# Local attention in a reordered round, and norms centred with the tokens on the partitions

## The chip, the cores and the metric

The kernel runs on one NeuronCore of a Trainium2 chip. The metric is the device time of one execution in microseconds (us), lower is better. A core has a matrix engine (PE, with weight loads shown apart as PEld), a vector engine (DVE), a scalar engine (ACT), a GpSimd engine (POOL) and a queue that issues transfers (SP). Each works through its own list of instructions; semaphores tie them together. Matrix products land in PSUM[...]; everything else lives in SBUF or in DRAM.

## The reference

Two blocks run one after the other on `x` of shape (2, 2048, 128), all in float32. Each block modulates a layer norm, adds an attention (kind A), modulates again and adds a stack of local-attention layers (kind B):

```python
h = layernorm(x) * (1 + ca) + sa;  x = x + ga * attn(h)
h = layernorm(x) * (1 + cb) + sb;  x = x + gb * local_layers(h)

# one local-attention layer (first block: 6 layers, 16 heads, window 32;
#                            second block: 2 layers, 8 heads, window 64; head size 64)
h = shift_token(x)                     # second half of the features comes from the token before
q, k, v = split(h @ Wqkv)
q, k = rotary_xpos(l2norm(q) * qs, l2norm(k) * ks)
o = softmax(mask(8 * q @ [k_prev_window, k_window].T)) @ [v_prev_window, v_window]
x = x + o @ Wo
h = layernorm(shift_token(x)) * g + b
a, gate = split(h @ W1 + b1)
x = x + (a * gelu(gate)) @ W2 + b2
```

The attention of the first block is a chunked delta-rule attention; that of the second is a causal linear attention with two layer norms and a feed-forward network of its own. Only the local-attention layers and the linear attention are touched by the change.

## The kernel before

The work is in three stages. `modulation` and `l0_attention` (up to about 530 us of the profile) do the first attention under an order written out by hand; the change does not touch them. `local_models` does all eight local-attention layers, with the linear attention of the second block threaded through the end of the sixth layer and the start of the seventh. In `local_models` a scheduler sets the final order of each engine's instructions from the order of the source, the data dependencies and the free buffers, so a round's instructions may interleave differently from round to round. Features lie on the partitions for the residual streams `hs[0]` and `hs[1]` (128 features by tokens).

A tile is 128 tokens of one of the two sequences, so a layer has 32 tiles, and the main loop runs one round per tile over a software pipeline. In round `i`, with `j = i + 3`:

- `scores(i + 1)` computes the masked scores into a two-bank PSUM tile (`wide`, line 991, mask in line 982), then DVE takes the maximum `mx` (line 999) and the difference `sm` (1001). `weights_exp` runs the exponential on ACT (1008), `weights_norm` the sum `rs` and its reciprocal on DVE (1015, 1016) and the product on POOL (1017).
- `project(j, 0)` and, for 16 heads, `project(j, 1)` compute 1,024 columns of queries and keys each into a `wide` tile (line 871). ACT squares them (`sq`, 873), DVE forms the two halves of the rotation, `r` (881) and `t` (886), and POOL adds them (892). After the last of a tile's projections DVE sums the squares (897) and runs `rsqrt_quick` (lines 167 to 180, last result `rq_y`), which uses the projection's own PSUM bank as scratch; POOL then scales `r` by `rq_y` (904). For 8 heads one projection holds queries and keys.
- `keys_first_(i)` turns the weights of tile `i` so that keys lie on partitions (`ps_pT`, line 1026), and ACT copies them (1027).
- `values(i + 2)` computes values (`ps_v`, line 951), ACT copies them into `vn`, and SP moves them window by window into `v2`, which has two buffers.
- `mix(i)` multiplies weights and values (`ps_o`, line 1043), ACT copies the outputs `on` (1049).
- `turn(i + 2, u)` turns queries and keys (`ps_turn`, line 923), ACT copies them to `qT` and `kT`, and the last window of the tile before is copied in front of the keys (line 934, or a memset in 932).
- `turn_out(i)` turns the outputs (`ps_oT`, line 1059), and `project_out(i)` multiplies them with `Wo` (`ps_y`, line 1071) and adds to the residual on DVE (1077).

`wide` tiles rotate through two pairs of banks, all others (`bank`) through four single banks. After every fourth tile of a sequence `feed_forward` queues six steps, of which each round runs two: `centre`, `variance`, `scale`, `gate`, `up`, `down`. `centre` multiplies 512 tokens with a centring matrix (line 1096), so features stay on the partitions, and squares the result on ACT (1098). `variance` sums the squares over the features with four one-column products on PE (1107) and takes the inverse root (DVE 1112, POOL 1114). `scaled` spreads that root over the partitions with four transposes on PE (1120), and DVE multiplies (1123). The linear attention and the last residual of a model queue steps in a second list, of which each round runs up to six (`lstep`); the linear attention calls `centre` and `variance` four times per 512 tokens, and `scaled` three times. The order of a round in the source is:

```python
            if i >= 0:
                keys_first_(i)
            if 0 <= i + 2 < n:
                values(i + 2)
            lstep()
            if i >= 0:
                mix(i)
            if 0 <= i + 2 < n:
                for u in range(len(layers[tiles[i + 2][0]][0].units)):
                    turn(i + 2, u)
            lstep()
            if i >= 0:
                turn_out(i)
```

In it stand both projections before `keys_first_(i)`.

Of the kernel before, what the change touches and what calls it, by code (L numbers as in the profile page):

```python
# [11 lines left out]
F32 = mybir.dt.float32  # L12
# [3 lines left out]
ALU = mybir.AluOpType  # L16
# [56 lines left out]
def tile_kernel(ctx: ExitStack, tc: tile.TileContext, a: dict, out: bass.AP):  # L73
# [634 lines left out]
    def local_models(mA, mB, hs0):  # L708
# [12 lines left out]
        def bank(name):  # L721
            return psT.tile([128, 512], F32, tag="T", name=f"ps_{name}")
# [139 lines left out]
        def project(i, u):  # L862
# [31 lines left out]
            if u == len(units) - 1:  # L894
# [7 lines left out]
                for v in range(len(units)):  # L902
# [2 lines left out]
                        rv, rv, bc(y[:, 16 * v:16 * v + 16].unsqueeze(2), (128, 16, DH)), ALU.mult  # L905
                    )

        def turn(i, u):

            g, b, t = tiles[i]  # L910
            m, _ = layers[g]
            W, NPR = m.W, m.NPR
            if u == 0:
                q = wk.tile([128, 1024], F32, name="qT")
                st[i]["q"] = q[:, 0:NPR * 128].rearrange("p (c i) -> p c i", c=NPR)
                k = wk.tile([128, 1280], F32, name="kT", bufs=3)
                st[i]["k"] = k[:, 0:NPR * (W + 128)].rearrange("p (c i) -> p c i", c=NPR)
            r = st[i].pop(("r", u))
            for e, (s, pb) in enumerate(m.units[u]):
                p = bank("turn")  # L920
                for c in range(4):
                    cs = slice(512 * e + 128 * c, 512 * e + 128 * c + 128)
                    nc.tensor.transpose(p[:, c * 128:(c + 1) * 128], r[:, cs], ident)  # L923
                pv = p.rearrange("p (c i) -> p c i", c=4)
                if s == 0:
                    nc.scalar.copy(st[i]["q"][:, 4 * pb:4 * pb + 4, :], pv)
                else:
                    nc.scalar.copy(st[i]["k"][:, 4 * pb:4 * pb + 4, W:W + 128], pv)  # L928
            if u == len(m.units) - 1:
                k = st[i]["k"]  # L930
                if t == 0:
                    nc.gpsimd.memset(k[:, :, 0:W], 0.0)
                else:
                    nc.scalar.activation(
                        k[:, :, 0:W], m.last_k[b][:, :, 128:128 + W], AF.Identity, scale=m.back
                    )
                m.last_k[b] = k

        def values(i):
            g, b, t = tiles[i]  # L940
# [150 lines left out]
                lsteps.pop(0)()  # L1091


        def centre(S, x, pool, keep):
            p = bank("c")
            nc.tensor.matmul(p, lhsT=cen, rhs=x, start=True, stop=True)  # L1096
            S["sq"] = pool.tile([128, 512], F32, name="fsq")
            nc.scalar.activation(S["sq"], p, AF.Square)
            if keep:
                S["xc"] = pool.tile([128, 512], F32, tag="t1", name="xc")  # L1100
                nc.scalar.copy(S["xc"], p)

        def variance(S, pool):
            p = bank("var")
            sq = S.pop("sq")
            for j in range(4):
                nc.tensor.matmul(  # L1107
                    p[:, j:j + 1], lhsT=sq[:, j * 128:(j + 1) * 128], rhs=onesm[:, 0:1],
                    start=True, stop=True,
                )  # L1110
            ve = pool.tile([128, 4], F32, name="fve")
            nc.vector.tensor_scalar(ve, p[:, 0:4], 1e-5, None, ALU.add)
            S["rt"] = pool.tile([128, 4], F32, name="frt")
            nc.gpsimd.tensor_tensor(S["rt"], ve, bc(nhalf, (128, 4)), ALU.pow)

        def scaled(S, x, out):
            p = bank("r")
# [121 lines left out]
        def linear(b, k):  # L1239
# [13 lines left out]
                pass  # L1253

            def a3():
                xc = S.pop("xc")
                scaled(S, xc, xc)
                h = S["h"] = lw.tile([128, 512], F32, name="h")
                nc.scalar.activation(
                    h, xc, AF.Identity, bias=mB[:, 0, b:b + 1], scale=mB[:, 1, b:b + 1]  # L1260
                )


# [132 lines left out]

            def f3():
                n0 = k * 512
                xc = S.pop("xc")
                scaled(S, xc, xc)  # L1400
                for lo, sh in ((0, 0), (64, 1)):
                    nc.scalar.activation(
                        hs0[lo:lo + 64, b, n0 + sh:n0 + sh + 512], xc[lo:lo + 64, :],
                        AF.Identity, bias=mB[lo:lo + 64, 3, b:b + 1],
                        scale=mB[lo:lo + 64, 4, b:b + 1],
                    )
                ready.add((b, k))
# [46 lines left out]
        for i in range(-3, n):  # L1454
            j = i + 3
            lstep()
            if 0 <= i + 1 < n:
                scores(i + 1)
                weights_exp(i + 1)
                weights_norm(i + 1)  # L1460
            more = False
            if j < n:
                g, b, t = tiles[j]
                jj = j % per
                nu = len(layers[g][0].units)
                more = g < last
                if g == second and t % 4 == 0:
                    while (b, t // 4) not in ready:
                        lstep()
                project(j, 0)  # L1470
                if more and jj == 4:
                    load_proj(g + 1, 0)
                if more and jj == 6 and g + 1 == second:
                    models[1].consts()
                if jj == 6 and g == second - 1:
                    linear_consts()
                if more and jj == 8:
                    factors(g + 1)
                    if 2 == 2:
                        load_out(g + 1)  # L1480
                if more and jj == 18:
                    load_ff(g + 1)
                if more and jj == 22:
                    fold_ff(g + 1)
                if more and jj == per - 1:
                    load_proj(g + 1, 1)
                lstep()
            step()
            if j < n and nu == 2:
                project(j, 1)  # L1490
                if more and jj == per - 1 and g + 1 < second:
                    load_proj(g + 1, 2)
            if j < n and b == B - 1 and j + 1 < n:
                tables(*tiles[j + 1][::2])
            lstep()
            if i >= 0:
                keys_first_(i)
            if 0 <= i + 2 < n:
                values(i + 2)
            lstep()  # L1500
            if i >= 0:
                mix(i)
            if 0 <= i + 2 < n:
                for u in range(len(layers[tiles[i + 2][0]][0].units)):
                    turn(i + 2, u)
            lstep()
            if i >= 0:
                turn_out(i)
            step()
            lstep()  # L1510
            if i >= 0:
                g, b, t = tiles[i]
                project_out(i)
                if 2 == 1 and i % per == per - 1 and g < last:
                    load_out(g + 1)
                if t % 4 == 3:
                    feed_forward(g, b, t // 4)
# [74 lines left out]
```

## Time and profile before

| what | us |
|---|---|
| median of three runs | 5040.5 |
| lowest and highest | 5033.6, 5043.1 |
| the profiled execution, its own time | 5053.3 |
| its span, first to last instruction | 5051.4 |
| first attention ends, local layers begin | about 530 to 614 |
| layers of 16 heads alone | 614 to 3590 |
| 16 and 8 heads, mixed with linear attention | 3590 to 4404 |
| layers of 8 heads alone | 4404 to 4990 |

The profile shows one execution. A row has the engine, the source line, the operation, the tiles it writes and reads, its shape, and how often it occurs. A number in square brackets behind a row is the time for which the engine stood idle before it, and what released it. A float32 product appears in the trace as two records, a transpose as one.

### The profile page before, as it was taken

The numbers are of one execution on the slowest core, as the hardware profiler recorded it, in microseconds if no ns is written. First come the engines' busy times: TensorE is split into PE (matmuls) and PEld (weight loads), VectorE is DVE, ScalarE is ACT, GpSimd is POOL, SyncE is SP. The second block draws the span as 40 slices with busy tenths as digits, with TensorE's granted clock in tenths as the row PEclk, the third lists the DMA queues.
The fourth block names the chain that finished last, engine by engine and source line by source line (L and its number), as shares of the span: only waits on it lengthen the run. The fifth ranks groups of instructions, "written<-read, shape, count | busy, mean of one in ns | idle before, by whom it ended". The sixth has DMA issues, their size and how long they took to land.

```text
span 5051.4 us, 171478 instructions
## 1 busy us (share of the span) xinstructions
PE 4682.5 (93%) x75042; PEld 3190.3 (63%) x75042; DVE 3883.5 (77%) x6760; ACT 2796.3 (55%) x4645; POOL 2761.1 (55%) x1650
## 2 busy tenths in 40 slices
PE   5667799999999999999999999999999998999998
PEld 4445566666666666666666666666666665566565
DVE  6993488788887887788887788787767766688886
ACT  3323356666666665566665566566555654555554
POOL 3331366666665666566666666665544533355553
PEclk8777799999999999999999999999999999999999
DMA  2000222222222322232222322232222211111111
GB/s 76 1 1 24 83 69 66 63 71 74 70 63 63 82 70 63 62 81 72 63 64 65 81 67 64 64 82 64 52 53 54 54 44 36 41 46 48 53 54 40
DMA packets 222491, 295.63 MB, mean 59 GB/s; under 512 B 75657, under 2 KB 95409, under 8 KB 221745
## 3 DMA queue, kind: packets, MB, share of 16 engines
q1 hardware_dynamic: 221744, 284.67, 21.8%
q8 instruction: 592, 9.70, 0.8%
q14 instruction: 155, 1.26, 0.1%
HBM read 40.98 MB, written 10.75 MB: 10 GB/s over the span
## 4 chain that ended last, share of the span: by engine, by line
PE 75%; DVE 6%; ACT 4%; issue 2%; POOL 2%; DMA 0%; SPq 0%; ACTq 0%; POOLq 0%; DVEq 0%
PE ps_qk L871 15%; PE ps_y L1071 8%; PE ps_turn L923 8%; PE ps_o L1043 7%; PE ps_s L991 7%; PE ps_v L951 6%; PE ps_f L1141 6%; PE ps_oT L1059 4%; PE ps_pT L1026 4%; PE ps_fy L1166 3%; PE ps_var L1107 1%; PE ps_c L1096 1%; PE ps_s L982 1%; POOL r L892 1%; ACT sq L873 1%
## 5 line engine op out<-in xcount | busy, mean ns | idle before, releaser
L892 POOL TENSOR_TENSOR r<-r,t 128x1024 f32<-128x1024 f32 x448 | 1059.9, 2366 | 1162.4 <-DVE t L886 1075.2
L873 ACT ACTIVATE sq<-ps_qk 128x1024 f32<-128x1024 f32 x448 | 459.1, 1025 | 1369.4 <-PE ps_qk L871 1353.2
L904 POOL TENSOR_TENSOR r<-r,rq_y 128x1024 f32<-128x1024 f32 x448 | 845.5, 1905 | 268.0 <-DVE rq_y L180 267.1
L871 PE MATMUL ps_qk<-wp,hs 128*128 128x512 f32 x1792 | 883.6, 616 | 30.1 <-DVE rq_y L180 15.4
L886 DVE TENSOR_TENSOR t<-ps_qk,tb 128x1024 f32<-128x1024 f32 (+1 forms) x512 | 552.8, 1080 | 180.5 <-POOL r L892 180.4
L1017 POOL TENSOR_TENSOR sm<-sm,rs 128x1024 f32<-128x1024 f32 x256 | 488.0, 1906 | 293.6 <-DVE rs L1016 196.2
L881 DVE TENSOR_TENSOR r<-ps_qk,tb 128x1024 f32<-128x1024 f32 (+1 forms) x512 | 547.7, 1070 | 103.1 <-ACT sq L873 102.1
L897 DVE TENSOR_REDUCE ps_qk<-sq 128x16 f32<-128x1024 f32 x448 | 549.6, 1227 | 13.5
L871 PEld LDWEIGHTS ps_qk<-wp,hs 128*128 128x128 f32 x1792 | 311.6, 191 | 351.5 <-issue 260.2
L1071 PEld LDWEIGHTS ps_y<-oT,wo 128*128 128x128 f32 x3584 | 440.8, 193 | 122.4 <-issue 71.1
L1071 PE MATMUL ps_y<-oT,wo 128*128 128x128 f32 x3584 | 482.8, 282 | 18.7 <-ACT oT L1060 18.2
L923 PE MATMUL ps_turn<-ident,r 128*128 128x128 f32 x3584 | 470.6, 281 | 22.9 <-issue 12.0
L1043 PEld LDWEIGHTS ps_o<-v,pT 64*32 64x32 f32 (+1 forms) x26624 | 343.6, 108 | 226.9 <-ACT pT L1027 114.9
L951 PE MATMUL ps_v<-wp,hs 128*128 128x512 f32 x896 | 446.9, 598 | 5.9 <-ACT o L1436 3.7
L999 DVE TENSOR_REDUCE mx<-ps_s 128x16 f32<-128x1024 f32 (+1 forms) x256 | 312.9, 1222 | 166.4 <-PE ps_s L991 162.1
L1043 PE MATMUL ps_o<-v,pT 64*32 64x64 f32 (+1 forms) x26624 | 392.5, 222 | 41.0 <-ACT pT L1027 23.3
L923 PEld LDWEIGHTS ps_turn<-ident,r 128*128 128x128 f32 x3584 | 395.2, 143 | 54.4 <-issue 15.8
L991 PE MATMUL ps_s<-kT,qT 64*32 64x64 f32 (+1 forms) x26624 | 400.5, 230 | 3.9 <-ACT kT L928 3.2
L1049 ACT COPY on<-ps_o 128x512 f32<-128x512 f32 x448 | 244.4, 589 | 244.1 <-PE ps_o L1043 244.1
L991 PEld LDWEIGHTS ps_s<-kT,qT 64*32 64x32 f32 (+1 forms) x26624 | 330.1, 107 | 70.3 <-issue 37.3
L1141 PE MATMUL ps_f<-fx,w 128*128 128x512 f32 (+1 forms) x768 | 365.5, 600 | 2.6 <-DVE fx L1123 1.7
L1026 PEld LDWEIGHTS ps_pT<-ident,sm 128*128 128x128 f32 x2048 | 245.7, 142 | 149.6 <-issue 142.1
(266 smaller groups left out, 7693.6 us busy)
## 6 DMA issues: line engine op xcount, KB each, us to landing
v<-vn SPq DMA_DIRECT2D x1276, 128.0 KB
v<-vn SPq DMA_DIRECT2D x744, 64.0 KB
v<-vn SPq DMA_DIRECT2D x64, 256.0 KB
wp<-in_L_ffn_Wqkv SPq DMA_DIRECT2D x20, 512.0 KB
xD<-xb SPq DMA_DIRECT2D x24, 256.0 KB
xb<-xD SPq DMA_DIRECT2D x24, 256.0 KB
cs<-in_cos SPq DMA_DIRECT2D x128, 32.0 KB
cs<-in_sin SPq DMA_DIRECT2D x128, 32.0 KB
```

What stands on the lines that cost most here:

```text
L871: nc.tensor.matmul(pq[:, js], lhsT=hw, rhs=wts[g, u][:, js], start=True, stop=True)
L881: nc.vector.tensor_tensor(r[:, es].rearrange("p (h d) -> p h d", d=DH), pq[:, es].rearrange("p (h d) -> p h d", d=DH), bc(tb[:, 0, s].unsq ...
L886: nc.vector.tensor_tensor(t2[:, es].rearrange("p (h s d) -> p h s d", s=2, d=32), pq[:, es].rearrange("p (h s d) -> p h s d", s=2, d=32)[: ...
L892: nc.gpsimd.tensor_tensor(r, r, t2, ALU.add)
L897: nc.vector.tensor_reduce(pq[:, 16 * v:16 * v + 16], st[i].pop(("sq", v)).rearrange("p (h d) -> p h d", d=DH), AX.X, ALU.add,)
L904: nc.gpsimd.tensor_tensor(rv, rv, bc(y[:, 16 * v:16 * v + 16].unsqueeze(2), (128, 16, DH)), ALU.mult)
L923: nc.tensor.transpose(p[:, c * 128:(c + 1) * 128], r[:, cs], ident)
L951: nc.tensor.matmul(p, lhsT=hw, rhs=wv, start=True, stop=True)
L991: nc.tensor.matmul(sp[W * w:W * w + W, c0:c0 + 2 * W], lhsT=qT[64 * q:64 * q + 64, cc, W * w:W * w + W], rhs=kT[64 * q:64 * q + 64, cc, W ...
L1043: nc.tensor.matmul(po[s][W * w:W * w + W, co:co + 64], lhsT=pT[kp, q, c, W * w:W * w + W], rhs=v2[kp, w, co:co + 64], start=True, stop=True,)
L1071: nc.tensor.matmul(py[:, 0:128], lhsT=wts[g, "o"][:, c * NO + s, :], rhs=oT[:, s, c, :], start=(c + s == 0), stop=(c == 3 and s == NO - 1),)
L1141: nc.tensor.matmul(ps_[c][0:sz], lhsT=wts[g, "w1"][:, o:o + sz], rhs=S["x"], start=True, stop=True,)
```

## The change

The change does four things.

1. It reorders the round: weights of tile `i` are turned between the two projection halves (for 8 heads ahead of the only one), then come the outputs `mix(i)`, then `values(i + 2)`, `turn_out(i)` and last `turn(i + 2)`.
2. It takes the allocation of `kT` and the copy of the window before it out of `turn` into a function of its own, `halo`, called before the last projection half.
3. `centre` now takes the tokens as the stationary operand, in four products of 128 columns, so tokens lie on the partitions and features along the row. `variance` sums the squares with one DVE reduction along the row, in place of the four products.
4. Where the centred values are kept (two of the four norms of the linear attention), POOL scales them by the inverse root, and `normed` turns them back with four transposes, from which ACT reads directly; the transposes of the root and the DVE product fall away there. `scaled` stays for the other norms.

```diff
+        def halo(i):
+            g, b, t = tiles[i]
+            m, _ = layers[g]
+            W, NPR = m.W, m.NPR
+            k = wk.tile([128, 1280], F32, name="kT", bufs=3)
+            k = st[i]["k"] = k[:, 0:NPR * (W + 128)].rearrange("p (c i) -> p c i", c=NPR)
+            if t == 0:
+                nc.gpsimd.memset(k[:, :, 0:W], 0.0)
+            else:
+                nc.scalar.activation(
+                    k[:, :, 0:W], m.last_k[b][:, :, 128:128 + W], AF.Identity, scale=m.back
+                )
+            m.last_k[b] = k
...
         def centre(S, x, pool, keep):
             p = bank("c")
-            nc.tensor.matmul(p, lhsT=cen, rhs=x, start=True, stop=True)
+            for j in range(4):
+                js = slice(j * 128, (j + 1) * 128)
+                nc.tensor.matmul(p[:, js], lhsT=x[:, js], rhs=cen, start=True, stop=True)
...
         def variance(S, pool):
-            p = bank("var")
-            sq = S.pop("sq")
+            ve = pool.tile([128, 4], F32, name="fve")
+            nc.vector.tensor_reduce(
+                ve, S.pop("sq").rearrange("p (j d) -> p j d", j=4), AX.X, ALU.add
+            )
+            nc.vector.tensor_scalar(ve, ve, 1.0 / 128.0, 1e-5, ALU.mult, ALU.add)
+            rt = S["rt"] = pool.tile([128, 4], F32, name="frt")
+            nc.gpsimd.tensor_tensor(rt, ve, bc(nhalf, (128, 4)), ALU.pow)
+            if "xc" in S:
+                v = S["xc"].rearrange("p (j d) -> p j d", j=4)
+                nc.gpsimd.tensor_tensor(v, v, bc(rt.unsqueeze(2), (128, 4, 128)), ALU.mult)
+
+        def normed(S):
+            p = bank("n")
+            xc = S.pop("xc")
             for j in range(4):
-                nc.tensor.matmul(
-                    p[:, j:j + 1], lhsT=sq[:, j * 128:(j + 1) * 128], rhs=onesm[:, 0:1],
-                    start=True, stop=True,
-                )
...
+                js = slice(j * 128, (j + 1) * 128)
+                nc.tensor.transpose(p[:, js], xc[:, js], ident)
+            return p
...
-                project(j, 0)
+                if nu == 2:
+                    project(j, 0)
...
-                if more and jj == per - 1:
+                if nu == 2 and more and jj == per - 1:
                     load_proj(g + 1, 1)
                 lstep()
             step()
-            if j < n and nu == 2:
-                project(j, 1)
-                if more and jj == per - 1 and g + 1 < second:
+            if i >= 0:
+                keys_first_(i)
+            if 0 <= i + 2 < n:
+                halo(i + 2)
+            if j < n:
+                project(j, nu - 1)
+                if nu == 2 and more and jj == per - 1 and g + 1 < second:
                     load_proj(g + 1, 2)
-            if j < n and b == B - 1 and j + 1 < n:
-                tables(*tiles[j + 1][::2])
+                if nu == 1 and more and jj == per - 1:
+                    load_proj(g + 1, 1)
+                if b == B - 1 and j + 1 < n:
+                    tables(*tiles[j + 1][::2])
             lstep()
             if i >= 0:
-                keys_first_(i)
+                mix(i)
+            lstep()
             if 0 <= i + 2 < n:
                 values(i + 2)
             lstep()
             if i >= 0:
-                mix(i)
+                turn_out(i)
             if 0 <= i + 2 < n:
                 for u in range(len(layers[tiles[i + 2][0]][0].units)):
                     turn(i + 2, u)
-            lstep()
-            if i >= 0:
-                turn_out(i)
             step()
             lstep()
             if i >= 0:
```

## The prediction

> **What bounds the kernel now.** I read the page first: span, and how busy TensorE (PE) is.
>
> ```profile
> span 5051.4 us, 171478 instructions
> PE 4682.5 (93%) x75042; PEld 3190.3 (63%) x75042; DVE 3883.5 (77%) x6760; ACT 2796.3 (55%) x4645; POOL 2761.1 (55%) x1650
> ```
>
> It looks PE-bound. Next, busy time by stretch: layers of the 16-head model alone (614 to 3590 us), those mixed with linear attention (3590 to 4404), layers of the 8-head model alone (4404 to 4990).
>
> ```profile
> core 0: us, PE busy (x) PEld busy (x) DVE busy (x) ACT busy (x) POOL busy (x), PEclk, DMA share, GB/s
> 614.00:3590.00 2976.00, 2906.74 (x55644) 2002.27 (x55626) 2405.72 (x3921) 1810.71 (x2977) 1891.98 (x1098) 0.99 0.27 69
> 3590.00:4076.00 486.00, 462.05 (x7043) 316.90 (x7046) 347.82 (x602) 269.90 (x433) 237.35 (x142) 0.97 0.21 53
> 4076.00:4404.00 328.00, 294.70 (x2435) 194.56 (x2419) 207.00 (x449) 161.63 (x252) 124.33 (x85) 0.93 0.13 36
> 4404.00:4990.00 586.00, 555.83 (x5116) 353.19 (x5120) 492.71 (x1037) 340.79 (x547) 317.49 (x199) 1.00 0.18 50
> ```
>
> PE reads 95 to 98% in three of the four, but DVE stands at 81 and 84% in the first and the last. So I read single rounds in the timeline. A round without feed-forward work in the 16-head model:
>
> ```profile
> 2259.21 0.19 DVE L180 SCALAR_TENSOR_TENSOR rq_y<-ps_qk,rq_g 128x32 f32<-128x32 f32 x1
> 2259.74 1.98 PE L871 MATMUL ps_qk<-wp,hs 128*128 128x512 f32 x4
> ...
> 2262.83 1.22 DVE L881 TENSOR_TENSOR r<-ps_qk,tb 128x1024 f32<-128x1024 f32 x1 [0.32 <-ACT sq L873]
> ...
> 2268.87 1.22 DVE L886 TENSOR_TENSOR t<-ps_qk,tb 128x1024 f32<-128x1024 f32 x1 [1.32 <-POOL r L892]
> ...
> 2274.38 0.19 DVE L180 SCALAR_TENSOR_TENSOR rq_y<-ps_qk,rq_g 128x32 f32<-128x32 f32 x1
> ...
> 2274.81 0.70 PE L871 MATMUL ps_qk<-wp,hs 128*128 128x512 f32 x1
> ```
>
> To be seen: the round lasts 15.07 us (2259.74 to 2274.81), and each first projection starts only 0.24 to 0.34 us after DVE's `rq_y` has ended, because the inverse root is computed in the PSUM bank that this projection takes over. So the round is a loop over engines: projection, square (ACT), `r` and `t` (DVE), sum (POOL), the second `t` (which waited 1.32 us for POOL), two sums of squares, the root, the next projection. PE hides beside it. In the 8-head model the loop shows as a wait:
>
> ```profile
> 4601.90 0.17 DVE L180 SCALAR_TENSOR_TENSOR rq_y<-ps_qk,rq_g 128x16 f32<-128x16 f32 x1
> 4602.00 1.21 DVE L999 TENSOR_REDUCE mx<-ps_s 128x8 f32<-128x1024 f32 x1
> 4602.13 1.99 PE L871 MATMUL ps_qk<-wp,hs 128*128 128x512 f32 x4 [0.25 <-DVE rq_y L180]
> ...
> 4605.28 0.69 DVE L881 TENSOR_TENSOR r<-ps_qk,tb 128x512 f32<-128x512 f32 x1 [0.74 <-ACT sq L873]
> ```
>
> To be seen: `rq_y` comes first, and then projection and square (3.1 us) run while DVE does the softmax's `mx` and `sm` (2.5 us). That overlap is what I expect the change to break.
>
> **What the Trainium skill says.** (1) "PSUM — Partial Sum Buffer", Engine vs sequencer instructions: DVE, ACT and POOL queues are strict FIFO and matmuls start in program order; so an instruction that waits holds all behind it, and the issue order decides. (2) The same page, on bank collisions: two engines reading one bank are serialised by an added dependency. The trace agrees: `r` starts 0.04 us after `sq` ends. (3) "Perfetto Trace Analysis", Tensor Engine Instruction: a matmul's end is an estimate; so I count PE from start to start (two 512-column projections in four records: 1.82 us, not the 1.98 shown).
>
> **Prices, start to start, in us.** First projection pair 1.82, second 1.72, eight weight turns 0.87, values 0.86 to 0.95 each, outputs 1.51, query turns 1.80, output turns 0.87, `y` 1.88, mask 0.32, scores 1.42: 14.02 for a 16-head round. In the timeline the regular rounds last: without feed-forward 15.15, with centring and variance 16.40, with `r` and gate 17.04, with up and down 19.24. Built, the two programs' issue orders hold 46 of the first kind in the 16-head layers and 40 or 41 of each of the others.
>
> **Norms.** Variance: 96 groups of eight one-column records leave PE at about 0.80 a group (2286.28 to 2287.09), 77 in all. Centring: eight records of 128 columns at 0.117 (as in `y`) for two of 512 at 0.43: +0.08, +8 in all. DVE gains 96 sums of 128x512 at 0.70 (L367: 695 ns), +67, and loses 16 products of L1123 at 0.68, -11. POOL gains 16 products at about 1.05 (L516, 1066 ns), beside other work where POOL is 38 to 49% busy (124 of 328 and 237 of 486 us); were that cover gone, 17. Transposes in `normed` cost what those in `scaled` did.
>
> **The 16-head rounds.** With outputs before the query turns, `y` no longer waits for the copies of `oT`; that saves PE about 0.87 in rounds of the first two kinds. But the loop above has no such step. Plain round: the loop at its tightest (0.25 less) is 14.82, so -0.3, 46 times: -14. Centring round: its loop takes 15.0 plus 0.70 for the new DVE sum, 15.7, against PE's 15.1: -0.65, 40 times: -26. Gate round: PE did nothing but work, 17.04; outputs now follow the second projection at 4.85 us after the round's start while the weight copies end at 4.95: +0.2, 40 times: +8. Up-and-down round: in the changed issue order five output matmuls stand ahead of the second projection, where before a value matmul, a projection and another value matmul stood between turns and outputs.
>
> ```profile
> 2311.32 1.28 ACT L1008 ACT_TABLE_LOAD   x1
> ...
> 2312.79 0.93 PE L1026 MATMUL ps_pT<-ident,sm 128*128 128x128 f32 x7
> ...
> 2313.59 1.05 ACT L1027 COPY pT<-ps_pT 128x512 f32<-128x512 f32 x2
> ```
>
> PE is done with the turns at 2313.55, the copies (behind table load and exponential) end at 2314.64: PE stalls 1.1 with the projection, values, turns and scores queued behind. 41 times 1.05: +43. Sum **+11**, from -32 (no stall) to +51 (the loop gains nothing).
>
> **Moved at no cost.** `halo` (a POOL memset or an ACT product) keeps its place after the turn copies in ACT's order. The value copies come 1.5 to 2.5 later, and with them the ten (three for 8 heads) DMA commands a tile on SP; these waited for the outputs two tiles back already, and their data is due a round later (10 us or more, DMA share 0.13 to 0.27). The table loads behind them on SP are due a round later too, and `load_proj` for the second 8-head layer, which moves behind the projection, happens once. If this cover fails, one landing of 3 us per layer, 24.
>
> **Linear attention stage.** 44 variance groups, 0.72 net each, -32 where PE binds; stalls at outputs give back some 10: **-20**, from -40 to +5.
>
> **The 8-head rounds.** Here weight turns and outputs now come before the only projection, so scores end early and DVE's fixed order puts the next `mx`, `sm` (and in some rounds the variance sum and `rs`) ahead of the last steps of the root. Example, a centring round, DVE from its `mx`: 1.25 + two steps 0.45 + `sm` 1.23 + step 0.22 + variance sum 0.70 + three steps 0.65 + `rs` 1.25 + `rq_y` 0.2 = 5.9. Only then may the projection start: +1.82, square +1.2, so `r` starts at 9.05 and DVE has been idle for 2.9. Four products 2.6, sum 1.25, steps and sums into `hs` 1.25: 14.15, against 11.6 before. Worked the same way in the changed order, a cycle of eight is 108.1, against 97.7 before (4493.4 to 4591.1):
> - plain 12.25: `rq_y` at 4.0, square at 7.1, products 9.75, sum 11.0, steps. Then the centring round, 14.15.
> - gate, 16.3 and 15.6: `rq_y` at 4.5 and 3.8, products to 10.25 and 9.55, sum, steps, `hs` and `u` to 14.8 and 14.1, then the scores held 1.5.
> - up and down, 14.4 twice: `sm` 2.5, `u` 4.0, `rs` after table load and exponential 6.4, products 9.25, sum 10.5, steps and `hs` 3.9.
> - centring 10.9 and plain 10.05: these enter with `rq_y` done, so the overlap is kept.
> The scores held for `rq_y`'s bank are shown by no row; without that the cycle is about 105. Six cycles: +42 to +62, taken as **+55**; lower bound 0, if queues slip so that the overlap survives, upper +80.
>
> Sum: 11 - 20 + 55 = **+46**. The profiled execution took 5053.3 us (span 5051.4), 12.8 above the median of 5040.5; 5099 on its scale is 5086 on the median's.
>
> **Rivals.** (A) PE sets all: -77 + 8, and in 87 rounds 0.87 less of waiting for `oT`, -76: -145, 4896. For it: 93% PE. Against: `rq_y` just ahead of each projection. It decides if plain rounds fall below 14.5. (B) Not slower: the 8-head overlap survives because PE leads by a whole round; then 11 - 20 = -9, 5031. It decides if that cycle stays under 99 us. (C) All at the upper ends, +51 + 5 + 62: 5158.
>
> **Numbers.** My forecast 0.6 (own range 5045 to 5130), A 0.07, B 0.2, C 0.13. 0.2% is 10 us, about what a measurement tells from no change. B splits evenly between faster and the same: faster 0.17, same 0.10, slower 0.73. The range, 5008 to 5145, leaves out A and the top of C.
>
> **Right or wrong.** Right: 8-head cycles near 108 us with DVE idle before `r` on `sq`; PE idle before outputs on `pT` by about 40 in up-and-down rounds; plain rounds near 14.85; no `ps_var` rows. Wrong: 8-head rounds as short as before, or plain rounds near 14.

## The result, and the profile after

The changed kernel took 5071.29 us (median of 6 runs, 5064.6 to 5082.29), the kernel before 5041.82 us in the same comparison (6 runs, 5033.6 to 5050.61). The ratio is 1.006, with a 95% interval of 1.0045 to 1.0075: slower by 29.5 us, against 46 forecast. The profiled execution took 5073.89 us.

The top of the page of the changed kernel:

```profile
span 5072.1 us, 170859 instructions
PE 4591.6 (91%) x74850; PEld 3154.3 (62%) x74850; DVE 3984.3 (79%) x6840; ACT 2861.4 (56%) x4645; POOL 2781.8 (55%) x1666
...
PE 52%; DVE 21%; ACT 7%; POOL 6%; issue 3%; DMA 1%; POOLq 0%; DVEq 0%; SPq 0%; ACTq 0%
```

The last line is the chain that ended last: the steps that, followed back from the end of the kernel, each released the next. In the kernel before it reads:

```profile
PE 75%; DVE 6%; ACT 4%; issue 2%; POOL 2%; DMA 0%; SPq 0%; ACTq 0%; POOLq 0%; DVEq 0%
```

To be seen: PE has 91 us less to do (4682.5 before) and the kernel is slower all the same. DVE has 101 us more. PE's share of the chain falls from 75% to 52%, and that of DVE rises from 6% to 21%. The busy time by stretch, with the columns and bounds of the prediction:

```profile
614.00:3590.00 2976.00, 2864.40 (x55493) 1986.86 (x55494) 2457.08 (x3949) 1856.66 (x2974) 1892.35 (x1098) 0.99 0.27 69
3590.00:4076.00 486.00, 434.98 (x6763) 300.22 (x6749) 348.56 (x585) 263.98 (x416) 240.77 (x149) 0.95 0.20 50
4076.00:4404.00 328.00, 283.20 (x2576) 192.36 (x2577) 224.84 (x471) 164.87 (x259) 130.18 (x89) 0.93 0.14 38
4404.00:4990.00 586.00, 534.88 (x5029) 347.98 (x5028) 498.96 (x1030) 346.85 (x540) 314.97 (x199) 0.99 0.18 49
```

To be seen: PE is less busy in every stretch, by 27.1 and 11.5 us in the two with linear attention. Work left PE; waiting took its place. These bounds are fixed times, though, and at a given time the two kernels are not at the same round.

To place it I cut every trace at the same tiles, each time where PE goes on from a tile's scores to its next work: the 16-head layers, the part with linear attention, the 8-head layers alone. The code ahead of these is the same in both kernels, and its length differs from one execution to the next: the first local projection starts at 582.1 us in the profile of before and at 573.6 in that of after. So the stages are compared, not the spans. The table holds the two kernels and all experiments (described below), in us. The four columns on the right are medians of one 16-head round, from the start of one tile's first projection to the start of the next one's. Each line comes from one execution; how far a stage differs between executions of one kernel was not measured.

| kernel | 16-head | linear | 8-head | plain | centring | gate | up-and-down |
|---|---|---|---|---|---|---|---|
| before | 2975.6 | 814.1 | 596.0 | 15.18 | 16.45 | 17.04 | 19.24 |
| after | 2983.1 | 828.9 | 600.7 | 14.87 | 16.41 | 17.24 | 20.19 |
| n_only | 2981.3 | 816.2 | 607.7 | 15.19 | 16.42 | 17.41 | 19.23 |
| r_only | 2975.8 | 826.6 | 613.8 | 14.87 | 16.03 | 17.12 | 20.19 |
| psum_ve | 2946.2 | 831.9 | 617.0 | 14.86 | 15.44 | 17.12 | 20.19 |
| strict | 2995.2 | 831.9 | 708.0 | 14.86 | 16.41 | 17.24 | 20.19 |
| pv | 2950.9 | 831.0 | 607.1 | 14.87 | 15.65 | 17.08 | 19.57 |
| t2b | 2918.5 | 818.5 | 598.0 | 14.66 | 15.14 | 17.12 | 20.19 |
| rest3 | 2986.1 | 804.2 | 619.5 | 14.87 | 16.41 | 17.24 | 20.19 |
| best2 | 2942.7 | 810.9 | 596.8 | 14.87 | 15.61 | 17.08 | 19.57 |
| b_t2b | 2971.9 | 798.5 | 596.9 | 15.19 | 16.47 | 17.05 | 19.24 |
| best3 | 2924.2 | 793.1 | 597.0 | 14.58 | 15.42 | 17.12 | 20.20 |
| best4 | 2922.2 | 796.3 | 596.1 | 14.60 | 15.60 | 17.08 | 19.58 |

After against before: +7.5 in the 16-head layers (forecast +11), +14.8 in the linear stage (forecast -20), +4.7 in the 8-head layers (forecast +55); together 27.0 of the 29.5. The sign was right, and two of the three terms were wrong. The third came out near by errors that cancel, which the medians hide. In sums over rounds 8 to 169, plain rounds rise by 2.9 us (forecast -14), centring rounds fall by 12.5 (-26), gate rounds rise by 2.3 (+8) and up-and-down rounds by 10.2 (+43). One reason is gaps of PE that the profile marks "issue": PE stands idle and the profile shows nothing that it waits for. In up-and-down rounds they shrink from 21.7 to 2.1 us in sum, and in plain rounds they grow from 1.3 to 12.5.

A plain 16-head round in the timeline of the changed kernel:

```profile
1704.85 0.19 DVE L180 SCALAR_TENSOR_TENSOR rq_y<-ps_qk,rq_g 128x32 f32<-128x32 f32 x1
1705.10 1.98 PE L871 MATMUL ps_qk<-wp,hs 128*128 128x512 f32 x4 [0.31 <-DVE rq_y L180]
...
1714.20 1.23 DVE L886 TENSOR_TENSOR t<-ps_qk,tb 128x1024 f32<-128x1024 f32 x1 [1.31 <-POOL r L892]
...
1719.71 0.19 DVE L180 SCALAR_TENSOR_TENSOR rq_y<-ps_qk,rq_g 128x32 f32<-128x32 f32 x1
...
1719.96 0.70 PE L871 MATMUL ps_qk<-wp,hs 128*128 128x512 f32 x1
```

To be seen: 14.86 us from projection to projection, as forecast; and now PE's record shows the wait for `rq_y` (0.31), which in the round shown of the kernel before it did not. The 8-head layers are another matter. This is a centring round:

```profile
4627.56 1.22 DVE L1005 TENSOR_TENSOR sm<-ps_s,mx 128x1024 f32<-128x1024 f32 x1
...
4629.07 1.88 PE L871 MATMUL ps_qk<-wp,hs 128*128 128x512 f32 x4
...
4631.09 0.16 DVE L180 SCALAR_TENSOR_TENSOR rq_y<-ps_qk,rq_g 128x16 f32<-128x16 f32 x1
...
4632.11 0.69 DVE L881 TENSOR_TENSOR r<-ps_qk,tb 128x512 f32<-128x512 f32 x1 [0.70 <-ACT sq L873]
```

To be seen: the projection starts 0.29 us after `sm` has ended and 2.0 us **before** `rq_y`. I had put it behind `rq_y`. DVE stands still for 0.70 us ahead of `r`, not for 2.9.

Last, why the median centring round gained next to nothing. `variance` now ends on DVE with a step that multiplies by 1/128 and adds 1e-5 (line 1115), 128x4 values from SBUF to SBUF. First a usual centring round, then one of the five short ones:

```profile
2567.21 1.92 POOL L1021 TENSOR_TENSOR sm<-sm,rs 128x1024 f32<-128x1024 f32 x1
2568.43 0.68 DVE L1112 TENSOR_REDUCE fve<-fsq 128x4 f32<-128x512 f32 x1
...
2569.07 2.37 POOL L892 TENSOR_TENSOR r<-r,t 128x1024 f32<-128x1024 f32 x1
...
2570.16 1.31 DVE L1115 TENSOR_SCALAR fve<-fve 128x4 f32<-128x4 f32 x1
```

```profile
1731.91 0.16 DVE L1115 TENSOR_SCALAR fve<-fve 128x4 f32<-128x4 f32 x1
...
1731.99 2.37 POOL L892 TENSOR_TENSOR r<-r,t 128x1024 f32<-128x1024 f32 x1
```

To be seen: the step takes 0.16 us when it starts before POOL's sum, and 1.31 us when it starts within it, ending 0.03 us after POOL (2571.47 against 2571.44). The reduction ahead of it isn't held although POOL is at work too (2568.43, within 2567.21 to 2569.13). All 59 long ones (over 0.3 us) of the 96 end within 0.2 us of the end of a POOL instruction. And the rounds follow it: of the 41 centring rounds among rounds 8 to 169, the 36 with a long step last 16.40 us or more, the five with a short one 15.31 to 15.44, with DVE's instructions around the step in the same order. The Trainium skill has this in "SBUF — State Buffer", Who interferes with whom: DVE and GpSimd share a pair of SBUF ports under an exclusive lock held for a whole instruction; a `tensor_scalar` can take a mode that needs the pair, a `tensor_reduce` on this chip cannot. The trace agrees on both. I had not read that page against the new line: before, this step read PSUM and took 0.15 us.

### The profile page after: what moved, and what is told of

Read it like the earlier page. It is cut to its first block, busy times and chain, and to the rows that moved or that the text cites. A ratio compares the mean times of both kernels' runs of the same rounds, so it can differ in the third digit from the quotient of the medians.

```text
span 5072.1 us, 170859 instructions
## 1 busy us (share of the span) xinstructions
PE 4591.6 (91%) x74850; PEld 3154.3 (62%) x74850; DVE 3984.3 (79%) x6840; ACT 2861.4 (56%) x4645; POOL 2781.8 (55%) x1666
## 3 DMA queue, kind: packets, MB, share of 16 engines
q1 hardware_dynamic: 221744, 284.67, 21.6%
## 4 chain that ended last, share of the span: by engine, by line
PE 52%; DVE 21%; ACT 7%; POOL 6%; issue 3%; DMA 1%; POOLq 0%; DVEq 0%; SPq 0%; ACTq 0%
PE ps_qk L871 12%; PE ps_turn L936 5%; PE ps_y L1075 5%; PE ps_v L955 5%; PE ps_o L1047 4%; PE ps_f L1156 4%; DVE t L886 4%; DVE ps_qk L897 4%; POOL r L892 4%; PE ps_s L995 4%; PE ps_fy L1181 3%; PE ps_oT L1063 3%; ACT sq L873 3%; DVE r L881 3%; DVE rs L1019 2%
## 5 line engine op out<-in xcount | busy, mean ns | idle before, releaser
L1047 PEld LDWEIGHTS ps_o<-v,pT 64*32 64x32 f32 (+1 forms) x26624 | 357.9, 108 | 281.9 <-ACT pT L1031 158.3
L1047 PE MATMUL ps_o<-v,pT 64*32 64x64 f32 (+1 forms) x26624 | 422.9, 223 | 58.5 <-ACT pT L1031 32.4
L955 PE MATMUL ps_v<-wp,hs 128*128 128x512 f32 x896 | 461.7, 631 | 1.0 <-issue 1.0
L936 PE MATMUL ps_turn<-ident,r 128*128 128x128 f32 x3584 | 448.3, 278 | 7.3 <-POOL r L904 5.8
L1075 PE MATMUL ps_y<-oT,wo 128*128 128x128 f32 x3584 | 447.1, 277 | 1.9 <-ACT oT L1064 1.9
L936 PEld LDWEIGHTS ps_turn<-ident,r 128*128 128x128 f32 x3584 | 411.5, 144 | 13.4 <-POOL r L904 10.6
L995 PE MATMUL ps_s<-kT,qT 64*32 64x64 f32 (+1 forms) x26624 | 366.5, 229 | 0.6 <-issue 0.6
L995 PEld LDWEIGHTS ps_s<-kT,qT 64*32 64x32 f32 (+1 forms) x26624 | 317.3, 107 | 62.1 <-issue 46.1
L1031 ACT COPY pT<-ps_pT 128x512 f32<-128x512 f32 x512 | 273.8, 585 | 143.3 <-PE ps_pT L1030 143.0
L1019 DVE TENSOR_REDUCE rs<-sm 128x16 f32<-128x1024 f32 (+1 forms) x256 | 310.0, 1211 | 53.9 <-ACT sm L1012 53.2
```

The lines of the kernel that those rows point to most:

```text
L955: nc.tensor.matmul(p, lhsT=hw, rhs=wv, start=True, stop=True)
L995: nc.tensor.matmul(sp[W * w:W * w + W, c0:c0 + 2 * W], lhsT=qT[64 * q:64 * q + 64, cc, W * w:W * w + W], rhs=kT[64 * q:64 * q + 64, cc, W ...
L1047: nc.tensor.matmul(po[s][W * w:W * w + W, co:co + 64], lhsT=pT[kp, q, c, W * w:W * w + W], rhs=v2[kp, w, co:co + 64], start=True, stop=True,)
L1075: nc.tensor.matmul(py[:, 0:128], lhsT=wts[g, "o"][:, c * NO + s, :], rhs=oT[:, s, c, :], start=(c + s == 0), stop=(c == 3 and s == NO - 1),)
```

## The experiments

### The two halves of the change apart

n_only is the kernel before with the functions `centre`, `variance`, `normed`, `a3` and `f3` of after. r_only is the kernel after with those functions of before.

> The norms of the change alone, in the round order of before. Theory (norms pay on DVE and POOL what they save on PE): in the linear attention stage PE waits for POOL's product ahead of the transposes of normed (47 us of PE idle in the changed kernel), so that stage gets longer by 5 to 20 us; centring rounds stay near 16.4 because the second variance step costs 1.3 us on DVE there; whole kernel 5030 to 5065, about 5045. Rival (the norms are the gain, the order the loss): centring rounds near 15.3, linear stage shorter, whole kernel 4990 to 5015.

> The round order of the change alone, with the norms of before. Theory (16-head rounds: plain -0.3, gate +0.2, up and down +0.95; long rounds of before mostly gone; 8-head cycle about as before): 16-head stage +5 to +20, linear stage within 10 of before, 8-head stage -5 to +5, whole kernel 5045 to 5065, about 5055. Rival (the order carries the whole +29.5): 5068 to 5075, with the linear stage some 15 us longer than before too. If it stays under 5040, the order is a gain and the norms are the loss.

Measured: n_only 5064.7 us (5 runs), ratio to before 1.0041 (1.0028 to 1.0054). r_only 5080.28 us (6 runs), 1.0071 (1.0057 to 1.0085). Each half alone is a loss, and neither expectation fits by stages. The total of n_only lies at the upper edge of its range, that of r_only above the ranges of theory and rival. In the linear stage the halves add up: +2.1 with the norms alone and +12.5 with the round order alone, together 14.6 of the 14.8. Between the same rounds PE's busy time falls there by 29.2 us in n_only, and its idle time grows by 31.6. In r_only work falls by 1.0, and idle time grows by 13.2. The largest waits of PE over 3590 to 4420 us, in n_only and in r_only:

```profile
PE ps_n L1123 <- POOL xc L1115: 29.9, 13, 4.4
PE ps_r L1130 <- POOL frt L1112: 10.7, 5, 3.6
```

```profile
PE ps_r L1125 <- POOL frt L1119: 38.1, 14, 4.8
```

(The numbers are us in total, times, and the longest in us.) In the kernel before, PE's waits for POOL's `frt` come to 21.6 us there. So each half makes PE wait longer for POOL: the norms at the turning back of the product `xc`, the order at the transposes of the root `frt`.

The 8-head layers lose in both halves (+11.7 and +17.8) and yet only 4.7 together, so there the halves do not add up. In r_only the centring rounds are 16.03, better than the 16.41 with both halves: there the new norms cost more than PE saved. In n_only the step of the norms (line 1110 there) is long in all of its 41 centring rounds:

```profile
L1110 DVE TENSOR_SCALAR fve<-fve x96: 157/1310/2652, 747.7 to 5042.5; 128x4 f32<-128x4 f32 x96
```

(Durations are shortest, median and longest in ns.)

### psum_ve: is it the shared port?

```diff
+            p = bank("var")
             nc.vector.tensor_reduce(
-                ve, S.pop("sq").rearrange("p (j d) -> p j d", j=4), AX.X, ALU.add
+                p[:, 0:4], S.pop("sq").rearrange("p (j d) -> p j d", j=4), AX.X, ALU.add
             )
-            nc.vector.tensor_scalar(ve, ve, 1.0 / 128.0, 1e-5, ALU.mult, ALU.add)
+            nc.vector.tensor_scalar(ve, p[:, 0:4], 1.0 / 128.0, 1e-5, ALU.mult, ALU.add)
```

> The changed kernel, with the sum of the variance written to a PSUM bank, so that the step after it (times 1/128, plus 1e-5) reads PSUM instead of SBUF; same instructions otherwise. Theory (that step, SBUF to SBUF, is held until a POOL instruction ends, 1.32 us instead of 0.16 in 36 of 41 centring rounds): it takes 0.15 to 0.2 us everywhere, centring rounds fall from 16.41 to 15.2 to 15.5, the linear stage loses another 5 to 15 us; whole kernel 5010 to 5030, about 5020. Rival (the 1.3 us lie beside the loop, which something else sets): the step shortens, centring rounds stay at 16.2 to 16.5, whole kernel 5065 to 5076.

Measured: 5051.01 us (22 runs), ratio to before 1.0016 (1.0008 to 1.0024), some 20 us below the change. The step by its line, after and in psum_ve:

```profile
L1115 DVE TENSOR_SCALAR fve<-fve x96: 157/999/2226, 751.4 to 5048.4; 128x4 f32<-128x4 f32 x96
```

```profile
L1116 DVE TENSOR_SCALAR fve<-ps_var x96: 149/162/163, 756.8 to 5032.5; 128x4 f32<-128x4 f32 x96
```

With the same work and PSUM as its source, the longest is 163 ns. Of the 96 steps 34 start within POOL's sum or its scaling by `rq_y`, and none of them is held: it is the source in SBUF that counts, which agrees with the lock. Centring rounds fall to 15.44, and the 16-head layers by 36.9 us. This fall alone would not name the cause, since the plan moved too: in all 41 centring rounds the step now stands among the last steps of the root, where POOL does nothing. That the hold sets these rounds is told by the five short ones of the change (15.31 to 15.44), which agree. The total was missed because the linear stage, expected 5 to 15 us shorter, got 3.0 longer, and the 8-head layers 16.3. Their plan changed (the sum takes a bank of PSUM, which it did not before), and there PE now stands in front of the transposes of `scaled`, which wait for POOL's `frt`. PE's waits in the 8-head layers (4404 to 4990 us), after and in psum_ve:

```profile
PE ps_r L1135 <- POOL frt L1117: 2.5, 3, 1.1
PE ps_qk L871 <- DVE rq_y L180: 1.7, 4, 0.5
```

```profile
PE ps_r L1136 <- POOL frt L1118: 19.8, 12, 2.8
```

17.3 us more of that wait, for 16.3 us of stage. The same wait stands at 10.1 us in r_only and at 9.4 in n_only, beside the larger losses of these two. That the stage is sensitive to where two instructions of a norm fall is a likely reading; no run takes this wait away by itself.

### strict: why the 8-head overlap survived

```diff
         def wide(name):
+            turn_of[0] ^= 1
-            return psA.tile([128, 1024], F32, tag="A", name=f"ps_{name}")
+            return psA.tile([128, 1024], F32, tag=f"A{turn_of[0]}", name=f"ps_{name}", bufs=1)
```

> The changed kernel, with the two bank pairs handed out in strict turn instead of to whoever asks when one comes free. Theory (my prediction's 8-head step failed because the projection takes the pair that sm has just freed, not the one of the last root): now it has to wait for the root of the projection before, and the 8-head cycle of eight rounds goes from 95.7 to 104 to 110 us, 8-head stage +40 to +80, linear stage longer too, 16-head rounds unchanged (plain 14.87, gate 17.24, up and down 20.19); whole kernel 5115 to 5170, about 5135. Rival (the overlap survived because queues slip, whatever the banks): 8-head cycle 94 to 98, whole kernel 5065 to 5080.

Measured: 5190.2 us (4 runs), 1.0293 (1.0279 to 1.0306); the medians of the four kinds of 16-head rounds unchanged, the 8-head layers +107.3 us, the cycle of eight 122.0 and 120.6 us where the change has 95.7. PE's waits for the root in the 8-head layers (4420 to 5000 us):

```profile
PE ps_qk L874 <- DVE rq_y L180: 28.9, 19, 3.2
```

1.7 us there in the change, 28.9 here. Of 44 projections of these layers, 19 start before the last root is done in the change; in strict, as in the kernel before, none does. So it is the free hand-out of the two pairs that lets an 8-head projection overtake the last root. The size is more than I expected, and not the price of the wait alone: the scheduler also moved the projection back in PE's issue order, mostly behind the turns of the outputs. What the wait alone costs stays open.

### pv: the stall ahead of the outputs

psum_ve, with `values(i + 2)` placed ahead of `mix(i)` again.

> The variance sum in PSUM as in psum_ve, and values placed ahead of mix again (round otherwise as changed). Theory (in up-and-down rounds five output matmuls wait 1.05 us for the weight copies with the second projection behind them; with a value matmul and that projection in between, the wait is covered): up-and-down rounds fall from 20.19 to 19.2 to 19.5, some 30 to 38 us; gate and centring rounds within 0.3 of psum_ve; 8-head rounds are planned anew, +-15; whole kernel 5005 to 5035, about 5018. Rival (something else in these rounds sets the 20.19, such as table load and exponential for the next scores): they stay above 20.0, whole kernel 5045 to 5060.

Measured: 5049.54 us (21 runs), 1.001 (1.0 to 1.0019), the same as psum_ve. The median of the up-and-down rounds falls by 0.62 to 19.57, just above the theory's range. So the wait for the weight copies was real, and two thirds of what these rounds had lost come back. PE's record had shown less of it: 19.7 us in 42 waits in the change, 0.47 a round. Here it shows none. But the mean goes up, from 20.30 to 20.49: eight such rounds are now 2.0 to 5.4 us longer than the median, which in psum_ve and in the change is not seen. PE's record there says "issue", which names no engine. Before had them too: PE's largest waits of that kind over 614 to 3590 us are

```profile
PE ps_o L1043 <- issue: 16.5, 9, 2.6
...
PE ps_turn L923 <- issue: 12.0, 12, 2.4
```

in before, and in the change

```profile
PE ps_o L1047 <- issue: 18.4, 17, 2.2
```

That is why the up-and-down rounds, 0.95 slower in the median, cost the change only 10.2 us in sum (802.1 to 812.3 over the 40 of rounds 8 to 169): in before their mean already stood 0.81 above the median. In the change most of these gaps stand in plain rounds. What they are stays open.

### rest3: PE in front of transposes that POOL feeds

```diff
-                fetch, rest, a0, lambda: centre(S, S["x"], lw, True), lambda: variance(S, lw), a3,
+                fetch, rest, a0, lambda: centre(S, S["x"], lw, True), lambda: variance(S, lw), rest, a3,
...
-                rest, lambda: centre(S, S["x1"], lw, False), lambda: variance(S, lw), d4, e1, e2,
-                rest, lambda: centre(S, S.pop("x"), lw, True), lambda: variance(S, lw), f3,
+                rest, lambda: centre(S, S["x1"], lw, False), lambda: variance(S, lw), rest, d4, e1, e2,
+                rest, lambda: centre(S, S.pop("x"), lw, True), lambda: variance(S, lw), rest, f3,
```

> The changed kernel, with one empty step more between variance and the transposes that use its result, at three places of each linear attention block. Theory (that stage is 15 us longer than before because PE stands in front of transposes whose operand POOL has not finished: 47 us at normed, 10 more at scaled): these waits fall below 20 us together, the linear stage goes from 829 to 795 to 815, whole kernel 5040 to 5060. Rival (the stage is set by the number of steps a block needs, which 8-head tiles wait for): the waits fall, the stage stays at 825 to 845, whole kernel 5068 to 5085.

Measured: 5067.72 us (5 runs), 1.0036 (1.0022 to 1.005), 3.6 below the change, a difference within the intervals. The total misses the theory's range. PE's waits of that kind over 3590 to 4420 us, in before, after and rest3:

```profile
PE ps_r L1120 <- POOL frt L1114: 21.6, 11, 3.6
```

```profile
PE ps_n L1128 <- POOL xc L1120: 47.3, 14, 7.2
PE ps_r L1135 <- POOL frt L1117: 18.6, 5, 5.1
```

```profile
PE ps_n L1128 <- POOL xc L1120: 26.5, 10, 5.6
```

From 21.6 to 65.9 us by the change, and down to 26.5 with the steps apart; the linear stage goes from 828.9 to 804.2 us. But these 24.7 us are not the waits. PE's idle time between the same rounds falls only from 102.0 to 92.9: waits for DVE take their place, 24.2 us of them ahead of the transposes `ps_aT` of the linear attention, where the change has 0.5. The other 16.0 us are work of PE that went past the end of the stage, as the blocks have more steps: the first two pairs of 8-head tiles after it last 35.2 and 36.3 us instead of 23.5 and 27.4, 20.6 more. So the waits for POOL could be moved, but taking them away did not give their time back; the rival, that the number of steps sets the pace, is nearer.

### t2b and b_t2b: the loop over DVE and POOL

```diff
-            t2 = wk.tile([128, 1024], F32, name="t2", bufs=1)
+            t2 = wk.tile([128, 1024], BF16, name="t2", bufs=2)
```

In the changed kernel this is t2b, in the kernel before b_t2b.

> The changed kernel, with two buffers for t2 in place of one; to fit them t2 is bfloat16, so the second rotary product is rounded. Theory (a plain 16-head round is a loop over projection, square, DVE's products, POOL's sum and the root, in which the second t waits for POOL's first sum): that wait goes, plain rounds fall from 14.87 to 14.0 to 14.5, centring rounds from 16.4 to 15.4 to 16.1, gate and up-and-down rounds stay within 0.2; whole kernel 5000 to 5045, about 5022. Rival (PE or POOL's own work sets these rounds): plain rounds 14.8 to 14.9, whole kernel 5065 to 5078.

> The kernel before, with two bfloat16 buffers for t2 in place of one (the second rotary product is rounded). Theory now (in the round order of before PE sets the 16-head rounds too, since y waits for the copies of oT and centring rounds show PE busy throughout; the loop over DVE and POOL only runs level with it): plain rounds stay at 14.9 to 15.2, centring rounds at 16.2 to 16.5, whole kernel 5025 to 5048, about 5035. Rival (my prediction's opening: the loop sets plain rounds of before and PE hides beside it): plain rounds 14.5 to 14.8, centring rounds 15.9 or less, whole kernel 4995 to 5020.

Measured: t2b 4990.55 us (4 runs), 0.9889 (0.9873 to 0.9905), 81 us below the change. b_t2b 5028.76 us (14 runs), 0.997 (0.9958 to 0.9981). DVE's wait for POOL's sum ahead of `t` over 614 to 3590 us, in before and after:

```profile
DVE t L886 <- POOL r L892: 170.0, 129, 3.6
```

```profile
DVE t L886 <- POOL r L892: 164.8, 124, 3.7
```

With two buffers it is gone from both programs. In the order of before this changes no median of the 16-head rounds (15.19, 16.47, 17.05, 19.24). In the changed order it takes 64.6 us from that stage. PE's wait for the root, in the change and in t2b:

```profile
PE ps_qk L871 <- DVE rq_y L180: 61.3, 60, 3.6
```

```profile
PE ps_qk L871 <- DVE rq_y L180: 9.2, 6, 2.8
```

So in before PE set the 16-head rounds and the loop ran level with it; the change took PE down, and the loop stayed. Plain rounds stop at 14.66, not at 14.0 to 14.5: in 29 of the 40 PE's record shows no wait at all, and their median is 14.53, so its own work takes that long. The total is below the theory's range. Most of t2b's gain is in centring rounds (15.14): there the step of line 1115 starts in most of them with only 0.14 us of a POOL instruction left, and is held in 6 of 41, so the two causes are mixed in them. One thing is not equal: POOL's sum is shorter with a bfloat16 operand, 2.13 against 2.35 us in the median, so the runs do not tell the second buffer from the shorter sum. b_t2b's gain is mostly in the linear stage (-15.6).

### Put together: best2, best3, best4

best2: the changed round with values first, only in 16-head rounds without linear attention steps; tokens-first norms with the sum in PSUM only in the feed-forward of the 16-head model; all else as before. best3: the same with values after mix, and the two buffers of t2b. best4: best2 with those two buffers.

> What paid, put together: the changed round with values ahead of mix only in 16-head rounds without linear attention work, tokens-first norms with the sum in PSUM only in the feed-forward of the 16-head model, everything else as before. Theory (stages add up): 16-head stage 2975.6 before, 2946 in psum_ve, less 35 for the up-and-down stall: 2905 to 2920; linear stage 810 to 822 and 8-head stage 594 to 600 as before; whole kernel 4965 to 4995, about 4980. Rival (long rounds of other kinds take back what is gained, as PE has less slack): 16-head stage 2930 to 2955, whole kernel 5005 to 5030.

> best2 with values after mix, as in the change, and two bfloat16 buffers for t2 (the second rotary product is rounded). Theory (stages add up): 16-head stage as in t2b or a little better, 2905 to 2920; linear stage 808 to 820, 8-head stage 594 to 600; whole kernel 4965 to 4985, about 4975. Rival (in t2b linear and 8-head stages gained from t2 too, and lose it in the old order): linear stage 820 or more, whole kernel 4988 to 5000.

> best2 with two bfloat16 buffers for t2 (the second rotary product is rounded): as best3, but values ahead of mix. Theory (with the loop opened PE sets every 16-head round, and the up-and-down stall is what is left): up-and-down rounds 19.5, plain 14.6, centring 15.1 to 15.3, 16-head stage 2885 to 2905, whole kernel 4945 to 4970, about 4958. Rival (where the stall is gone, up-and-down rounds get PE's long issue gaps of 3 to 5 us instead, ten of them, as in pv and best2): their mean stays at 20.2 or more, 16-head stage 2912 to 2930, whole kernel 4972 to 4995.

Measured: best2 5010.13 us (5 runs), 0.9924 (0.9912 to 0.9937), in float32 throughout; best3 and best4 round the second rotary product, as t2b does. best3 4979.05 us (4 runs), 0.9875 (0.9859 to 0.989). best4 4973.37 us (4 runs), 0.9858 (0.9842 to 0.9874). All beat both kernels. Outside the 16-head layers they stand within 1 us of before or below it; the linear stage is even shorter in best3 and best4 (793.1 and 796.3), below the range of the theory, as in b_t2b. The 16-head stage of best3 lies 4 us above its range, and in best2 and best4 it follows the rivals: values first lowers the median of up-and-down rounds and brings the long gaps back (mean 20.41 and 20.42), so it gains next to nothing over best3.

## Why the prediction was right, and where it was wrong

**Slower by 46, measured 29.5: right in sign and range, by errors that cancel, so in part by luck.** The sum was 35 us too low in the linear stage and 50 too high in the 8-head layers, and within the 16-head term plain and centring rounds were too low and up-and-down rounds too high.

**What bounds the kernel now: wrong.** "PE hides beside it" does not hold for before: b_t2b takes the loop's wait away and no 16-head round moves. The 0.24 to 0.34 us between `rq_y` and the projection show that the loop kept up with PE, not that it set the pace. My sum of PE's prices (14.02 for a plain round) was about 0.5 too low as well: plain rounds of t2b in which PE waits for nothing last 14.53 in the median.

**Plain rounds, -0.3: right in the median, wrong in sum.** 15.18 to 14.87. The bound I named is that of the changed kernel, and t2b shows it. But the term of -14 counted every round at the tightest; with the "issue" gaps that came into plain rounds, the forty take 2.9 us more than before.

**Centring rounds, -0.65: failed.** Measured -0.04 in the median. The mis-sized term is the step after the new sum, taken as the row of before has it; it cost 1.32 us in the median, in a loop that has no slack. The five rounds in which it is not held last 15.31 to 15.44, 0.3 to 0.4 below what I had forecast.

**Gate rounds, +0.2: right** (+0.20). **Up and down, +1.05: right in kind and near in size** (+0.95, and pv takes 0.62 of it back). PE's record shows it as a wait for `pT` of 19.7 us in all, half of the 40 named as a sign; where the rest of the 0.95 lies stays open. Its worth over the stage was too high (10.2 us for 43), since "issue" gaps of before left these rounds at the same time.

**Linear stage, -20: failed.** PE did lose the work: 30.5 us between the same rounds, near the 32 reckoned. But its idle time grew by 45.2, and 44.3 of that is waiting for POOL (65.9 less 21.6). The term that failed is POOL's product, costed at nothing beside other work, with "transposes in `normed` cost what those in `scaled` did": the transposes stand at once behind a chain of square, sum, held step, root and product. n_only shows the outcome, +2.1 for the norms where -32 was put. The 10 that stalls at outputs were to give back are near what the round order alone costs (+12.5 in r_only), but the wait that grew there is that for `frt`; those at outputs did not grow. That the waits for POOL hold this stage alone is not shown, as in rest3 other waits took their place.

**8-head rounds, +55: failed, at "only then may the projection start".** The projection takes the pair of PSUM banks that `sm` has just freed. My own sign of being wrong came true: in the first 8-head layer the cycle of eight is 95.7 us, shorter than the 97.7 before, and in the round shown DVE waits 0.70 ahead of `r`, not 2.9. In the second layer it grows, from 100.6 to 104.2, for a reason that no run singles out. Without the free hand-out the case is real, as strict shows (122.0). Rival B had this part, and put 5031 because it shared my -20.

Rival A (PE sets all) put plain rounds below 14.5; even with the loop open their median stops at 14.6.

**Moved at no cost: held.** DMA stands at 1% of the chain that ended last, as against PE's 52%.

## What to carry to other kernels

Taking work from a full engine pays only down to the next loop, and whether that loop is close is told by removing its wait in the old program and in the new: here the same edit (a second buffer, with a shorter sum) changed no median of the 16-head rounds before the change and took 65 us from their stage after it, part of it in steps that were no longer held. Where rounds vary, add them up by kind; the median alone hid that the plain ones gained nothing. When an operation moves from PSUM to SBUF on DVE, look at what POOL does in that time, not only at the operation's row. And where a step feeds PE through POOL, count PE's wait for it: here the waits took more than the work that PE was spared, and moving the step later only brought other waits.

## What the runs showed of the hardware beyond what was expected

A DVE `tensor_scalar` of 128x4 values, SBUF to SBUF, took 0.16 us or up to 2.65, by what POOL was doing; from PSUM never over 0.164, also in the 34 cases of psum_ve that start within a sum or scaling of POOL. Not every POOL instruction held it: within POOL's inverse root of 128x4 values (line 1117 in after) three steps, one each in after, strict and t2b, started with 0.28 to 0.60 us of it left and took 0.16. POOL's sum of two 128x1024 operands took 2.35 us in the median with both in float32, and 2.13 us with one in bfloat16. PE shows gaps of up to 2.6 us marked "issue" in the 16-head layers of before, 21 of them ahead of outputs and query turns, and of up to 3.1 us in best4; they change their place with the order of the program, and no run here tells their cause.
